# Gate times up on VectorE straight from the PSUM bank, and an instruction order planned from traced durations

## The chip, the cores and the metric

One core of one Trainium2 chip. The time is device microseconds of one execution of the kernel on that core; the time before is the median of three executions. Engines are named as in the profile: PE is TensorE's matmuls and PEld its weight loads, DVE is VectorE, ACT is ScalarE, POOL is GpSimd, SP is SyncE, whose queue issues all transfers. A wait is written as "who <- whom".

## The reference

The input is x of 4 x 2048 x 256 in f32. Two residual blocks follow each other.

1. A layer norm, and then a Mamba block with a layer norm and a residual of its own: a projection to xi and z (512 channels each), a causal convolution of four taps and Silu that give u, a projection of u to dt, B and C, delta = softplus(dt W + b), and a scan over time with 64 states for each of the 512 channels, `h = h * exp(delta * A) + delta * u * B`, `y = sum over states of h * C`. Then y + u D, times silu(z), times W_out.
2. A layer norm and a feed-forward part with hidden size 768: `silu(x Wg) * (x Wu)`, times Wd, where the weights are integers times 1/127.

```
h = jax.nn.silu(gate) * up
return jnp.einsum('bsh,dh->bsd', h, wd)
```

The change sits in this last product, and in the order of everything.

## The kernel before

**Tiling.** Time is cut into 16 blocks n of 512 tokens (4 sequences of 4 blocks). In a block the scan has 512 channels times 64 states, which is 256 tiles of 128 partitions (2 channels by 64 states) by 512 steps. Sixteen tiles make a group; there are 256 groups in all. A group lives in one of three ring buffers, `ring`, of 16 x 512 floats per partition.

**One group** (function `group`):
- SP loads delta times u, repeated over 64 partitions, from a scratch in DRAM (`dusc`) into the ring, four transfers of 1 MB, and the exponents' pieces into `stk`.
- POOL multiplies by B, eight tiles in one instruction (L1524, 8.9 us), after it put the carried state into the first column (L1409) where a sequence goes on.
- For each tile, PE spreads delta over the partitions into one of four PSUM banks `a` (L1419), ACT makes exp(A delta) of it in place (L1425), and DVE runs the scan in the ring (L1430). ACT copies the last column into `carry` (L1440).
- PE contracts the 16 tiles with C (L1454, 128 small matmuls), ACT copies that (L1474), PE sorts it (L1487), ACT copies it to `yt` (L1498). Then the ring is free.

**Dense work** of neighbouring blocks is interleaved with the groups: `front`, `front_a` and `front_b` of block n+1 (layer norms, projections, convolution, Silu of u and z at L909 to L912, `softplus`), `back` of block n-1 (the gate with z and W_out), and `back_b` of block n-1, the feed-forward part. The layer norm's statistics are DVE's (L447, L448), its root goes through four small operations on ACT that end at L469, and DVE goes on at L472. `softplus` makes on ACT and POOL (L853, L855) the two summands that PE adds in a bank (L861), ACT copies the bank (L867), and DVE multiplies it by u (L868) into one of four buffers `w2`, which SP stores to `dusc`; the buffer is written again once the store is done. L1023 is DVE's gate of the scan's result, from a bank that PE filled at L999. The four `ps` banks of PSUM are shared by all dense work and the contraction.

**The feed-forward part** (`back_b`, 15 times; the last block has a version of its own, `back_last`): six projections for the gate, evicted by ACT (L1137), one Silu over all six (L1156, L1157, with the exponential's table loaded again at L1158), and six projections for up. Each of those is copied out of its bank by ACT into a `w2` buffer (L1144), and POOL multiplies the gate by it (L1146). Then the projection down (L1055).

**What sets the order.** No engine's order is written by hand. `Planner` takes every operation with an engine, a cost in ns and what it reads and writes; `run` keeps a clock for each engine and places one operation after another, the one that can start earliest, with a bias for its due step among the scans. Instructions are issued in that order, and each engine runs its own queue in order. So each cost (`SCAN`, `dve(n)`, `act(n)`, the figures in the `op` calls, `LAT` between engines, `WIRE` in bytes per ns for transfers) moves instructions. The ring products ("MUL") go to POOL in sets of eight, or singly to DVE in the first group alone. PE gets a decay matmul twice where the planner thinks it would otherwise be too little used (L1419 runs 5248 times for 4096 tiles).

Of the kernel before, what the change touches and what calls it, by code (L numbers as in the profile page):

```python
# [21 lines left out]
T = 512  # L22
# [7 lines left out]
NPS = 4  # L30
EXP_LN = "natural_log_exp_and_others"

LAT = {"PE": 195, "ACT": 137, "DVE": 150, "POOL": 150, "SP": 0, ("ACT", "PE"): 190, ("DVE", "DVE"): 130}
SLOPE = 17.0
LEAD = 170.0
LAG = -230.0
# [14 lines left out]
HOLD_TOL = 300.0  # L51
HOLD_ON = ("PE", "ACT")
WINDOW = 0
WIRE = 300.0
SCAN = 1130
TINY = 160


def lag(src, dst):
# [28 lines left out]
class Planner:  # L88
# [105 lines left out]
    def run(self, mul):  # L194
        clock = {e: 0.0 for e in ("PE", "ACT", "DVE", "POOL", "SP")}
        busy = dict(clock)
        wire = 0.0
        cols, recent = {}, deque()
        cur = 0
        self.ready = {e: [] for e in list(clock) + ["MUL"]}  # L200
        for o in self.ops:
            if not o.wait:
                self.ready[o.eng].append(o)
        left = len(self.ops)

        def bias(o):
            if o.kind == "S":
                return 0.0
            return max(LAG, min(LEAD, SLOPE * (o.step - cur)))

        while left:
            best = None
            for e, now in clock.items():
                pick = None
                cands = []
                due = 1e18
                for o in self.ready[e]:
                    t = self.allocatable(o, 2)
                    if t is None:
                        continue  # L220
                    t = max(now, o.est, t)
                    if e == "SP" and o.kind == "S":
                        t = max(t, wire - AHEAD)
                    if o.kind == "S":
                        due = min(due, t)
                    cands.append((o, t))
                for o, t in cands:
                    late = HOLD if e in HOLD_ON and o.kind != "S" and t + o.cost > due + HOLD_TOL else 0.0
                    sc = (t + bias(o) + late, o.idx)
                    if pick is None or sc < pick[0]:  # L230
                        pick = (sc, t, [o])
                if self.ready["MUL"] and (e == "POOL" or e == "DVE" and self.ready["MUL"][0].key[0][0] == 0):
                    m = min(self.ready["MUL"], key=lambda o: o.idx)
                    whole = m.key[0][0] == 0 or MUL_SET == sum(o.key[0] == m.key[0] for o in self.ready["MUL"])
                    if e == "POOL":
                        ms = sorted(
                            (o for o in self.ready["MUL"] if o.key[0] == m.key[0]), key=lambda o: o.idx
                        )
                        ms = [o for i, o in enumerate(ms) if o.key[2] == m.key[2] + i]
                        sc = 0.0  # L240
                    else:
                        ms = [m]
                        sc = max(LAG, min(MUL_LEAD, SLOPE * (m.step - MUL_MARGIN - cur)))
                    t = max(now, max(o.est for o in ms))
                    sc = (t + sc, m.idx)
                    if whole and (pick is None or sc < pick[0]):
                        pick = (sc, t, ms)
                if pick and (best is None or pick[1] < best[1]):
                    best = (e, pick[1], pick[2])
            assert best, "no instruction can be placed"  # L250
            e, t, os = best
            if os[0].eng == "MUL":
                cost = 120 + 1092 * len(os) if e == "POOL" else 690
                mul(e, os)
                clock[e] = end = t + cost
                busy[e] += cost
                for o in os:
                    self.ready["MUL"].remove(o)
                    o.eng = e
                    self.commit(o, t, end)  # L260
                left -= len(os)
                continue
            o = os[0]
            self.ready[e].remove(o)
            cost, times = o.cost, 1
            if e == "PE":
                i = int(t / TICK)
                if cols.get(i - 1, 0) < WARM:
                    cost *= 2
                n = o.cols or o.cost * 2.4  # L270
                while recent and recent[0][0] < t - TICK:
                    recent.popleft()
                if o.key == "decay" and sum(c for _, c in recent) < KEEP:
                    times = 2
                    cost *= 2
                    n *= 2
                recent.append((t + cost, n))
                i = int((t + cost) / TICK)
                cols[i] = cols.get(i, 0) + n
            if e == "SP":  # L280
                clock[e] = t + 625
                wire = max(wire, t + 1275) + o.cost
                end = wire + 985
                busy[e] += o.cost
            else:
                clock[e] = end = t + cost
                busy[e] += cost
            if o.key == "scan":
                cur += 1
            self.commit(o, t, end)  # L290
            for _ in range(times):
                o.fn()
            left -= 1
        return clock, busy
# [25 lines left out]
def mamba_ffn_kernel(  # L320
# [74 lines left out]
    nc.gpsimd.memset(cz.rearrange("p a b c -> p (a b c)"), 0.0)  # L395

    def dve(n=T, ptr=False, fast=False):
        return 140 + n * (0.52 if fast else 1.0417) + (61 if ptr else 0)

    def act(n=T, psum=False, ptr=0):  # L400
        return n * 0.834 + (70 if psum else 110) + 93 * ptr
# [7 lines left out]
    def tok(t):  # L409
        return t.t.rearrange("p a t -> p (a t)").rearrange("p (s c) -> p s c", s=4)  # L410
# [14 lines left out]
    def layer_norm(src, blocks=range(4), twice=False):  # L425
# [18 lines left out]

        def stats(j, s):
            st = buf("bst")
            op("DVE", 402, lambda: nc.vector.bn_stats(st.t, tok(src)[:, s, :]), [(src, s // 2)], [st])  # L447
            op("DVE", TINY, lambda: nc.vector.bn_aggr(mv()[:, j, :], st.t), [st], [(lp, 0, j)])  # L448

        for j, s in enumerate(blocks):  # L450
            stats(j, s)
# [276 lines left out]
    def front_a(n):  # L728
# [4 lines left out]
        def ev_x(k):  # L733
# [4 lines left out]
            def ev(ps):  # L738
# [8 lines left out]

                def weigh(j):
                    op(
                        "PE", 1220,  # L750
                        lambda: nc.tensor.matmul(  # L751
                            ps.t, dg.t[:, j * P : (j + 1) * P], xi.t[:, j : j + T], start=(j == 0), stop=(j == 3)
                        ),
                        [(xi, 0), (xi, 1), dg], [ps],
                    )
# [78 lines left out]
    def softplus(n, m):  # L834
# [14 lines left out]
        def ev(ps):  # L849
# [7 lines left out]

            def add(t):
                op(
                    "PE", 1220,  # L860
                    lambda: nc.tensor.matmul(ps.t, ident, t.t, start=False, stop=True, skip_group_check=True),  # L861
                    [t], [ps],
                )
# [35 lines left out]
    def front_b(n):  # L899
# [3 lines left out]
        if n:  # L903
# [7 lines left out]
                    nc.scalar.activation(szs[h].t, szs[h].t, AF.Silu)  # L911
                nc.scalar.preload_act_table_set(EXP_LN)  # L912

            op("ACT", 6240, silu, uk + zk, uk + zk)
        else:

            def silu_a():
# [10 lines left out]

        def mm_dt(k):
            return (  # L930
                240,
                lambda ps: nc.tensor.matmul(
                    ps[32 * k : 32 * k + 32, :], framed(wxp, k), u.t[:, k, :], start=True, stop=True
                ),
            )
# [174 lines left out]
    def back_b(n):  # L1110
# [29 lines left out]

        def ev_u(k):
            def ev(ps):
                up = buf("w2")
                op("ACT", act(T, True), lambda: nc.scalar.copy(up.t, ps.t), [ps], [up])  # L1144
                op(
                    "POOL", 1230, lambda: nc.gpsimd.tensor_tensor(hm(k), hm(k), up.t, ALU.mult),  # L1146
                    [up, hk[k]], [hk[k]],
                )

            return ev  # L1150

# [5 lines left out]
            nc.scalar.activation(hmb.t, hmb.t, AF.Silu)  # L1157
            nc.scalar.preload_act_table_set(EXP_LN)  # L1158

        op("ACT", 5300, silu, hk, hk)  # L1160
        for k in range(6):
            project(wgu, HID + k * P, xT, ev_u(k), [("wgu", 1, k)])
        wdk = [("wd", c, k) for c in range(2) for k in range(3)]
# [160 lines left out]
    def carry_over(n, h):  # L1324
# [22 lines left out]
        def c0(j):  # L1347
# [13 lines left out]
            [ps], xk[0:2], step=at,  # L1361
        )
        op(
            "POOL", 460, lambda: nc.gpsimd.tensor_tensor(ck2, ck2, c0(0), ALU.mult),
            xk[0:2] + ck, ck, step=at,
        )
        op(
            "POOL", 460, lambda: nc.gpsimd.tensor_tensor(ck2, ck2, c0(1), ALU.add),
            xk[2:4] + ck, ck, step=at,
        )  # L1370

    def group(G):
# [32 lines left out]
                load_du(a, m)  # L1405
        if not first:
            op(
                "POOL", 250,
                lambda: nc.gpsimd.tensor_copy(ring.t[:, :, 0], carry[:, g * 16 : g * 16 + 16]),  # L1409
                [("carry", g)], heads,  # L1410
            )
# [52 lines left out]
        for hb in range(2):  # L1464
            pm = buf("ps")
            for j in range(4):
                r8 = hb * 4 + j
                op(
                    "PE", 592, unit(pm, r8), keys + czk, [pm], step=s0 + 1 + C_PACE * r8,
                    after=[last["ext"]] if "ext" in last else [], cols=1024,  # L1470
                )

            def evac(hb=hb, pm=pm):
                nc.scalar.copy(  # L1474
# [17 lines left out]
                        stop=(jl == 1),  # L1492
                    )

        last["ext"] = op("PE", 592, ext, [(mm, 0), (mm, 1), "exs"], [ex], alloc=[yt], step=s0 + 18, cols=1024)

        def put():
            nc.scalar.copy(  # L1498
# [95 lines left out]
```

## Time and profile before

| | |
|---|---|
| median of 3 executions | 5084.1 us (5080.46 to 5089.4) |
| profiled execution | 5088.69 us, span of its instructions 5086.9 us |
| granted TensorE clock, mean | 0.968 |
| DMA | 1299.85 MB, 256 GB/s over the span, queue q1 67.4% of 16 engines' time |
| steady part, 130 to 4965 us | DVE busy 4614.06, POOL 4648.86, ACT 3833.08, PE 4248.31 of 4835.0 |
| gate copies by ACT, L1144 | 90 of 594 ns |
| gate products by POOL, L1146 | 90 of 1275 ns |

How to read what follows: a group's line gives line, engine, operation, tiles written and read, shapes and count, then busy us and mean ns of one, then the engine's idle time just before them and what ended most of it. A wait's line gives the total in us, how often, and the longest. In a timeline the two first numbers are start and length in us, a bracket is idle time just before and who ended it.

### The profile page before, as it was taken

The page shows a single profiled execution, that of the slowest core. Times are in us where ns is not written, and L with a number is a line of the kernel's source. Part 1 is how long each engine was busy: PE and PEld are TensorE (multiplying, and loading weights), DVE is VectorE, ACT ScalarE, POOL GpSimd, SP SyncE. Part 2 cuts the span into 40 slices and gives each one's busy share as a digit, 9 for nine tenths or more (in the row PEclk, how much of TensorE's full clock was granted, in tenths as well). Part 3 has the DMA queues.
Part 4 walks back from the last instruction along what each step waited for, and adds up shares of the span by engine and source line. Part 5 has one row for each costly group of instructions (what it writes and reads, how often), then busy time and mean ns, then how long its engine had stood idle before and what let it go on. Part 6 is the DMA issues. An engine that isn't in the chain of part 4 may idle for free. (4 is left out here: it accounts for less than half of the span.)

```text
span 5086.9 us, 115635 instructions
## 1 busy us (share of the span) xinstructions
PE 4443.6 (87%) x46946; PEld 2210.7 (43%) x46946; DVE 4769.4 (94%) x4681; ACT 3985.9 (78%) x7158; POOL 4764.7 (94%) x917
## 2 busy tenths in 40 slices
PE   7879898998988989889998888988889898898888
PEld 3334353443534435344443544435344353443435
DVE  5999999999999999999999999998999999999996
ACT  7777878878787787877878788777887878878674
POOL 4999999999999999999999999998999999999994
PEclk8999999999999999999999999989999999999999
DMA  7666776676776667767677776667766676666762
GB/s 265 258 251 250 259 274 264 245 277 241 277 275 235 257 254 286 279 245 277 242 269 258 276 279 244 267 237 258 267 250 267 241 284 255 249 258 246 274 243 88
DMA packets 306345, 1299.85 MB, mean 256 GB/s; under 512 B 33617, under 2 KB 134737, under 8 KB 174866
## 3 DMA queue, kind: packets, MB, share of 16 engines
q1 hardware_dynamic: 305810, 1292.44, 67.4%
q8 instruction: 369, 6.05, 0.5%
q14 instruction: 166, 1.36, 0.1%
HBM read 1186.94 MB, written 105.38 MB: 254 GB/s over the span
## 5 line engine op out<-in xcount | busy, mean ns | idle before, releaser
L1430 DVE TENSOR_TENSOR_SCAN ring<-a,ring 128x512 f32<-128x512 f32 x4096 | 4599.2, 1198 | 163.1 <-ACT a L1425 104.7
L1524 POOL TENSOR_TENSOR ring<-ring,b 128x4088 f32<-128x4088 f32 (+2 forms) x512 | 4538.7, 8894 | 86.0 <-DMA ring<-dusc 59.4
L1425 ACT ACTIVATE a<-a,a 128x512 f32<-128x512 f32 x4096 | 2686.0, 665 | 749.2 <-PE a L1419 715.5
L1419 PE MATMUL a<-stk,selb 128*128 128x512 bf16 x5248 | 1846.1, 395 | 460.9 <-DVE ring L1430 423.7
L1454 PE MATMUL ps<-ring,cz 128*32 128x128 f32 x32768 | 1223.8, 280 | 27.8 <-issue 19.7
L1419 PEld LDWEIGHTS <-selb 128*128 128x128 bf16 x5248 | 495.6, 99 | 1488.9 <-issue 1390.3
L1454 PEld LDWEIGHTS ps<-ring,cz 128*32 128x32 f32 x32768 | 818.9, 110 | 587.4 <-issue 525.6
L523 PE MATMUL ps<-w,wgu 128*128 128x512 f32 x720 | 372.3, 600 | 0.1
L1474 ACT COPY mm<-ps 128x512 f32<-128x512 f32 x512 | 302.7, 592 | 71.8 <-PE ps L1454 70.7
L1487 PE MATMUL ps<-mm,exs 128*32 128x128 f32 x4096 | 285.3, 408 | 13.2 <-ACT mm L1474 12.8
L523 PE MATMUL ps<-w,win 128*128 128x512 f32 x512 | 262.2, 597 | 0.0
L751 PE MATMUL ps<-xi,w 128*128 128x512 f32 x480 | 250.7, 604 | 0.0
L1487 PEld LDWEIGHTS ps<-mm,exs 128*32 128x32 f32 x4096 | 117.0, 119 | 204.8 <-ACT a L1425 75.0
L1055 PE MATMUL ps<-wd,w 128*128 128x256 f32 x720 | 181.2, 381 | 0.0
L523 PEld LDWEIGHTS ps<-w,wgu 128*128 128x128 f32 x720 | 136.8, 192 | 96.4 <-issue 52.2
L855 POOL TENSOR_TENSOR w<-w,w 128x512 f32<-128x512 f32 x63 | 81.3, 1290 | 101.3 <-ACT w L853 101.3
L861 PE MATMUL ps<-w,ident 128*128 128x512 f32 x252 | 147.2, 669 | 31.6 <-ACT w L854 21.1
L1146 POOL TENSOR_TENSOR w<-w,w 128x512 f32<-128x512 f32 x90 | 113.2, 1275 | 42.2 <-ACT w L1144 42.1
L1055 PEld LDWEIGHTS ps<-wd,w 128*128 128x128 f32 x720 | 135.6, 190 | 31.1 <-issue 4.8
L523 PEld LDWEIGHTS ps<-w,win 128*128 128x128 f32 x512 | 98.7, 193 | 74.8 <-issue 43.4
L1055 PE MATMUL ps<-wout,w 128*128 128x256 f32 x480 | 127.0, 383 | 1.3 <-ACT ps L1070 1.0
L751 PEld LDWEIGHTS ps<-xi,w 128*128 128x128 f32 x480 | 86.5, 189 | 78.7 <-issue 70.8
(138 smaller groups left out, 2407.2 us busy)
## 6 DMA issues: line engine op xcount, KB each, us to landing
ring<-dusc SPq DMA_DIRECT2D x1023, 1024.0 KB, 7.0
stk<-dsc SPq DMA_DIRECT2D x256, 96.0 KB, 3.8
qd<-w SPq DMA_DIRECT2D x32, 512.0 KB, 8.4
szd<-w SPq DMA_DIRECT2D x32, 512.0 KB, 8.3
dusc<-w SPq DMA_DIRECT2D x63, 256.0 KB, 3.4
dsc<-pk SPq DMA_DIRECT2D x63, 256.0 KB, 3.5
rsum<-w SPq DMA_DIRECT2D x31, 512.0 KB, 4.2
w<-rsum SPq DMA_DIRECT2D x31, 512.0 KB, 7.2
```

Source lines behind the costliest of these rows:

```text
L523: lambda ps: nc.tensor.matmul(ps, w[:, c, o : o + P], xT.t[:, c, :], start=(c == 0), stop=(c == 1)),
L751: lambda: nc.tensor.matmul(ps.t, dg.t[:, j * P : (j + 1) * P], xi.t[:, j : j + T], start=(j == 0), stop=(j == 3)),
L861: lambda: nc.tensor.matmul(ps.t, ident, t.t, start=False, stop=True, skip_group_check=True),
L1055: lambda ps: nc.tensor.matmul(ps[:, (s % 2) * DM : (s % 2 + 1) * DM], src(k)[:, s * P : (s + 1) * P], w[:, k, :], start=False, stop=(k == ...
L1146: "POOL", 1230, lambda: nc.gpsimd.tensor_tensor(hm(k), hm(k), up.t, ALU.mult),
L1419: "PE", 216, lambda: nc.tensor.matmul(a.t, selb[:, p, :], stk.t, start=True, stop=True),
L1425: lambda: nc.scalar.activation(a.t, a.t, AF.Exp, scale=a2f[:, idx : idx + 1]), [a, "a2"], [a],
L1430: nc.vector.tensor_tensor_scan(v, a.t, v, 0.0, ALU.mult, ALU.add)
L1454: nc.tensor.matmul(pm.t[cg * 32 : cg * 32 + 32, (r8 % 4) * P : (r8 % 4 + 1) * P], framed(cz, blk), ring.t[:, :, blk * 8 : blk * 8 + 8], st ...
L1474: nc.scalar.copy(mm.t[:, hb * 4 : hb * 4 + 4].rearrange("p r a t -> p (r a t)"), pm.t)
L1487: nc.tensor.matmul(ex.t[jh * 32 : jh * 32 + 32, 0:P], framed(exs, jh * 2 + jl), mm.t[:, :, :, jh * 2 + jl], start=(jl == 0), stop=(jl == 1),)
L1524: e.tensor_tensor(v, v, b2.t[:, None, t0:].to_broadcast([P, m, T - t0]), ALU.mult)
```

## The change

The planner's figures are replaced: transfers at 390 bytes per ns for 300, a scan at 1115 for 1130, DVE's fixed part at 50 for 140, the layer norm's operations at 326, 205 and 60 for 402, 160 and 160, the convolution's and softplus's matmuls on PE at 860 for 1220, the Silus and some POOL operations, and a surcharge where PE goes from a decay matmul to one with narrow weights. The six up projections of `back_b` are no longer copied: DVE multiplies the gate by the bank itself. `back_last` did so already, in halves. Line numbers move: by five up to the feed-forward part (L868 becomes L873), not at all in the first part of `group` (L1425 and L1430), by two at its end (L1524 becomes L1526). The gate product is L1148.

```
-LAT = {"PE": 195, "ACT": 137, "DVE": 150, "POOL": 150, "SP": 0, ("ACT", "PE"): 190, ("DVE", "DVE"): 130}
+LAT = {"PE": 195, "ACT": 137, "DVE": 165, "POOL": 150, "SP": 0, ("ACT", "PE"): 190, ("DVE", "DVE"): 140}
...
-WIRE = 300.0
-SCAN = 1130
-TINY = 160
+WIRE = 390.0
+SCAN = 1115
+TINY = 60
+SWITCH = 90
...
-                cost = 120 + 1092 * len(os) if e == "POOL" else 690
+                cost = 88 + 1092 * len(os) if e == "POOL" else 690
...
+                if was == "decay" and o.key == "narrow":
+                    cost += SWITCH
+                was = o.key
...
-        return 140 + n * (0.52 if fast else 1.0417) + (61 if ptr else 0)
+        return 50 + n * (0.52 if fast else 1.0417) + (61 if ptr else 0)
...
-            op("DVE", 402, lambda: nc.vector.bn_stats(st.t, tok(src)[:, s, :]), [(src, s // 2)], [st])
-            op("DVE", TINY, lambda: nc.vector.bn_aggr(mv()[:, j, :], st.t), [st], [(lp, 0, j)])
+            op("DVE", 326, lambda: nc.vector.bn_stats(st.t, tok(src)[:, s, :]), [(src, s // 2)], [st])
+            op("DVE", 205, lambda: nc.vector.bn_aggr(mv()[:, j, :], st.t), [st], [(lp, 0, j)])
...
-                        "PE", 1220,
+                        "PE", 860,
...
-            op("ACT", 6240, silu, uk + zk, uk + zk)
+            op("ACT", 6400, silu, uk + zk, uk + zk)
...
-                240,
+                430,
...
         def ev_u(k):
             def ev(ps):
-                up = buf("w2")
-                op("ACT", act(T, True), lambda: nc.scalar.copy(up.t, ps.t), [ps], [up])
-                op(
-                    "POOL", 1230, lambda: nc.gpsimd.tensor_tensor(hm(k), hm(k), up.t, ALU.mult),
-                    [up, hk[k]], [hk[k]],
-                )
+                op("DVE", dve(), lambda: nc.vector.tensor_tensor(hm(k), hm(k), ps.t, ALU.mult), [ps, hk[k]], [hk[k]])
...
-        op("ACT", 5300, silu, hk, hk)
+        op("ACT", 5450, silu, hk, hk)
...
-            "POOL", 460, lambda: nc.gpsimd.tensor_tensor(ck2, ck2, c0(0), ALU.mult),
+            "POOL", 400, lambda: nc.gpsimd.tensor_tensor(ck2, ck2, c0(0), ALU.mult),
...
-                "POOL", 250,
+                "POOL", 150,
...
-                op(
-                    "PE", 592, unit(pm, r8), keys + czk, [pm], step=s0 + 1 + C_PACE * r8,
+                o = op(
+                    "PE", 560, unit(pm, r8), keys + czk, [pm], step=s0 + 1 + C_PACE * r8,
                     after=[last["ext"]] if "ext" in last else [], cols=1024,
                 )
+                o.key = "narrow"
...
-        last["ext"] = op("PE", 592, ext, [(mm, 0), (mm, 1), "exs"], [ex], alloc=[yt], step=s0 + 18, cols=1024)
+        last["ext"] = op("PE", 1045, ext, [(mm, 0), (mm, 1), "exs"], [ex], alloc=[yt], step=s0 + 18, cols=1024)
+        last["ext"].key = "narrow"
```

More of the change, by code (lines that the diff above doesn't have):

```diff
@@ L198, in run @@
         cols, recent = {}, deque()
+        was = None
         cur = 0
@@ L859, in add @@
                 op(
-                    "PE", 1220,
+                    "PE", 860,
                     lambda: nc.tensor.matmul(ps.t, ident, t.t, start=False, stop=True, skip_group_check=True),
@@ L1367, in carry_over @@
         op(
-            "POOL", 460, lambda: nc.gpsimd.tensor_tensor(ck2, ck2, c0(1), ALU.add),
+            "POOL", 400, lambda: nc.gpsimd.tensor_tensor(ck2, ck2, c0(1), ALU.add),
             xk[2:4] + ck, ck, step=at,
```

## The prediction

> **What bounds the kernel now.** I read the busy shares first, then the waits of VectorE (DVE) in the steady part, then the timeline around one place of each kind of wait. Busy shares and three groups:
>
> ```profile
> PE 4443.6 (87%) x46946; PEld 2210.7 (43%) x46946; DVE 4769.4 (94%) x4681; ACT 3985.9 (78%) x7158; POOL 4764.7 (94%) x917
> ...
> L1430 DVE TENSOR_TENSOR_SCAN ring<-a,ring 128x512 f32<-128x512 f32 x4096 | 4599.2, 1198 | 163.1 <-ACT a L1425 104.7
> L1524 POOL TENSOR_TENSOR ring<-ring,b 128x4088 f32<-128x4088 f32 (+2 forms) x512 | 4538.7, 8894 | 86.0 <-DMA ring<-dusc 59.4
> ...
> L1146 POOL TENSOR_TENSOR w<-w,w 128x512 f32<-128x512 f32 x90 | 113.2, 1275 | 42.2 <-ACT w L1144 42.1
> ```
>
> Two engines stand at 94%: DVE with the 4096 scans and GpSimd (POOL) with the products that the scans read. One follows the other through three ring buffers, so either can set the pace. A table by stage settles the steady part, 130 to 4965 us: of 4835.0 us DVE is busy 4614.1 and idle 220.9. The busy part is work that must be done; a change there is worth its duration, and everything else is worth what it takes from or adds to the 220.9. Its largest pieces, as waits of DVE in that stretch (total, times, longest):
>
> ```profile
> DVE ring L1430 <- ACT a L1425: 101.2, 61, 3.3
> DVE ring L1430 <- POOL ring L1409: 34.2, 23, 6.0
> DVE ps L472 <- ACT ps L469: 21.4, 7, 4.6
> DVE w L868 <- ACT pk L867: 15.1, 22, 2.4
> DVE w L868 <- ACT x L872: 14.2, 10, 3.3
> DVE ring L1430 <- POOL ring L1524: 7.5, 2, 3.8
> ```
>
> The first row splits by the timeline. At 15 places ScalarE runs the Silu of u and z (L909 to L912), at 15 more that of the feed-forward part (L1156 to L1158); with four `a` banks DVE runs dry there, 41.0 and 30.4 us in all. The other 29.8 us of the row are elsewhere. Most of the POOL waits (rows 2 and 6, 41.7 us) follow the second Silu. POOL there, between two sets of ring products:
>
> ```profile
> 649.40 1.27 POOL L1146 TENSOR_TENSOR w<-w,w 128x512 f32<-128x512 f32 x1
> 652.13 1.29 POOL L1146 TENSOR_TENSOR w<-w,w 128x512 f32<-128x512 f32 x1 [1.47 <-ACT w L1144]
> ...
> 654.46 8.87 POOL L1524 TENSOR_TENSOR ring<-ring,b 128x4088 f32<-128x4088 f32 x1
> 663.29 4.96 POOL L1146 TENSOR_TENSOR w<-w,w 128x512 f32<-128x512 f32 x4
> ```
>
> The reader sees six gate products in POOL's queue, one of them waiting for ScalarE's copy while ring products stand behind it. DVE then waits 0.80 us at 653.8 and 4.64 us at 673.3. POOL's lead over DVE, from the end of a ring set to its first scan, has a median of 3.9 us over the 255 later groups and falls to 0 after this place, period by period.
>
> **The change part by part.** The order of both builds, engine by engine, shows that it does what it says: 90 products move to DVE (DVE goes from 4683 to 4779 instructions, with six more ring products of the first group), 90 copies leave ScalarE, 90 products leave POOL, and 58 decay matmuls that only keep TensorE warm go.
>
> 1. Added work on DVE. A product of this form, 128x512 with one operand in a PSUM bank, lasts 688 ns (L1079). What one costs in line is less:
>
> ```profile
> 1045.48 5.66 DVE L1430 TENSOR_TENSOR_SCAN ring<-a,ring 128x512 f32<-128x512 f32 x5
> 1051.05 0.66 DVE L1023 TENSOR_TENSOR w<-ps,yl 128x512 f32<-128x512 f32 x1
> 1051.63 4.55 DVE L1430 TENSOR_TENSOR_SCAN ring<-a,ring 128x512 f32<-128x512 f32 x4
> ```
>
> Scan follows scan by 1.115 us (median of all such pairs), though one lasts 1.198; scan, product, scan is 1.697 between the scans without waits. So a product costs 0.582 us, and 90 cost **+52.4 us**. The Trainium skill ("VectorE: DVE Perf Modes", section "The DRAIN you can't avoid") states that the next operation starts only when the pipe is empty; the 1.115 against 1.198 disagrees. By that rule the price would be 90 x 0.688 = 61.9 us, 9.5 more.
> The six extra ring products (0.582 each, 3.5 us) lie before 80 us, where DVE also waits for transfers and POOL: +2, between 0 and 3.5.
>
> 2. New wait of DVE for the bank. Behind each waiting product stand the scans; behind those the `a` banks and TensorE. I counted in the order how many scans stand between the scan that frees the last decay bank ahead of the up matmul on TensorE and the product on DVE: none in 4 places, one in 22, two or more in 64. What must fit is a decay matmul (0.395), the second up matmul (0.600) and about 0.2 of signalling, 1.2 us, against 1.115 per scan. So 4 x 1.2 + 22 x 0.2 = **+9 us**; bounds 0 and 32 (the nearest rows, the L1023 products, wait 22.8 us in 64, and 90 x 0.36 = 32).
>
> 3. POOL is relieved of 113.2 us of products and 42.1 of waits in a queue that is 96% busy in the steady part (4648.9 of 4835.0). What goes on DVE are the 41.7 us, except those behind L855, which stays: **-36**, bounds -20 and -42. What is late next is the transfer: the start of a ring set comes 7.4 us at the least, 15.2 in the median, after the contraction that frees the ring, so POOL can run some 7 us further ahead before transfers stop it.
>
> 4. The layer norm's wait (L472, 21.4 us in 7). In the order before, exactly seven of these in the steady part have no scan between the last L448 and L472, so DVE stands through four operations of ScalarE. The new durations put 1, 2 or 14 scans there every time, and places with 1 or 2 do not wait now: **-21**, bounds -15 and -21.
>
> 5. Softplus's buffer. ScalarE waits 39.2 us for the store of w before it may write it again (L853), up to 4.6 us, and DVE runs dry behind it; that is most of the 29.8 us. From the scan of the store to the reuse there were five scans or fewer in 16 places and are in 5 after, six in 6 and 9. I take half: **-15**, bounds 0 and -30.
>
> 6. Waits of L868 and L1023 (30.8 and 12.6 in the steady part): distances are more even, with no clear gain; -5, bounds +20 and -20. The first gate product stands in the shadow of the second Silu in 8 of 15 places, where DVE is idle anyway: 8 x 0.582, **-5**.
>
> 7. Nothing for the 90 copies (53.1 us): ScalarE at 78% waits 715.5 us for decay matmuls, and those wait for DVE; if that cover went, the copies would be a gain of 53.1 at most. Nothing for 58 x 0.395 = 23 us of TensorE, which waits 423.7 us for scans. SP's 1904 entries are the same in number, another order of transfers; at 67.4% load I count nothing, and DMA waits of DVE were none in the steady part. The two Silus keep their 71.4 us less the 5. The tail after the last scan, 5032 to 5087, has the same operations in the same places.
>
> Sum: 52.4 + 2 + 9 - 36 - 21 - 15 - 5 - 5 = **-18.6 us**. The profiled execution took 5088.7 us (span 5086.9 and 1.8 around it), 4.6 over the median of 5084.1. So 5070.1 for an execution like the profiled one, and **5065** on the median's footing.
>
> **The rivals.**
> - *Slower.* DVE is the one bound, and waits only change cause: the POOL waits go (-36), but the new order makes as many stalls of ScalarE and TensorE as it takes away. 52.4 + 2 + 9 - 36 = +27, so 5111. It decides when less than 63 us of the 220.9 goes. For it: L868, L1023 and the Silus are not touched by the new durations. Against: the counts of points 4 and 5. 0.23.
> - *No change.* Half of points 4 to 6: -23 in place of -46, so about +4 and 5088, or 5075 to 5094 around it. 0.21.
> - *Much faster.* With POOL ahead and order and durations in step, most of the 149.5 us outside the Silus goes, say 120: 52.4 + 2 + 9 - 120 - 5 = -62, so 5022. For it: the lead of POOL that recovers. 0.13.
> - *On a rule.* The Trainium skill ("Perfetto Trace Analysis", section "Optimizing Scalar/DVE Operations") speaks against the change: when VectorE is saturated, work is to be taken off it, to ScalarE or GpSimd. The 94% of DVE agree, and by the rule alone the sum is the added products and no more, +52. The POOL wait rows are what it leaves out.
> - That the change isn't made as it says has no chance: the order shows the 90.
>
> **How the numbers follow.** Forecast 5050 to 5073: 0.43; much faster 0.13; no change 0.21; slower 0.23. Within 0.2% means 5073.9 to 5094.3, about what a measurement of this kernel can tell from no change. Faster is 0.43 + 0.13 = 0.56, same 0.21, slower 0.23. All worst ends together (52.4 + 3.5 + 32 - 20 - 15 + 20) give +73, 5157; all best (52.4 - 42 - 21 - 30 - 20 - 5) -66, 5018. The range of 5022 to 5118 leaves out the far ends of both.
>
> **What would show it.** Right: DVE busy up by about 52 to 62, its idle time in the steady part from 221 to 150; no POOL row over 10 us among DVE's waits; L472's row near 0; POOL near 92% and more of its idle time behind DMA. Wrong: a wait of the gate products on TensorE's bank well over 9 us, ScalarE's `a` row over 101.2 (ScalarE or TensorE became the pace), scans of more than 1.198 us, or a lower granted clock than 0.968.

## The result, and the profile after

The kernel became slower by 0.4%: 5105.3 us in the median of 6 runs (5101.94 to 5109.25), against 5085.1 of the kernel before (6 runs, 5080.45 to 5093.99). The ratio is 1.0039, 95% interval 1.0026 to 1.0052. The forecast was 5065, faster; the range of 5022 to 5118 held the time, the sign was wrong. The profiled execution took 5101.94 us (span 5100.1) at a granted clock of 0.974, against 5088.69 (5086.9) at 0.968.

The page after; the lines answer to the first fence of the prediction:

```profile
PE 4502.0 (88%) x46888; PEld 2159.3 (42%) x46888; DVE 4827.6 (95%) x4777; ACT 3939.5 (77%) x7068; POOL 4650.4 (91%) x827
...
L1526 POOL TENSOR_TENSOR ring<-ring,b 128x4088 f32<-128x4088 f32 (+2 forms) x512 | 4530.6, 8868 | 260.2 <-DMA ring<-dusc 185.8
L1430 DVE TENSOR_TENSOR_SCAN ring<-a,ring 128x512 f32<-128x512 f32 x4096 | 4607.2, 1194 | 110.4 <-ACT a L1425 65.0
```

DVE's busy time rose by 58.2 us. POOL fell to 91%, and its idle time ahead of the ring products went from 86.0 to 260.2 us, most of it behind the ring's loads: POOL no longer sets the pace. Before the scans DVE waits 110.4 us, not 163.1. So far everything is as forecast. The span grew by 13.2 us because 58.2 came and only 45.0 of DVE's 317.5 us of idle time went. In the steady part (130 to 4975 us after the change) its idle time fell from 220.9 us to 186.1; the prediction had named 150 as the sign of being right. None of the signs of being wrong that it named came. Where the idle time stayed, as waits of DVE from 130 to 4975 us (total, times, longest):

```profile
DVE ring L1430 <- ACT a L1425: 65.0, 51, 3.1
DVE ring L1430 <- issue: 29.0, 10, 3.2
DVE w L873 <- ACT x L877: 27.7, 20, 2.2
DVE w L873 <- ACT pk L872: 17.4, 13, 3.2
DVE ring L1430 <- POOL ring L1409: 11.9, 16, 2.5
DVE w L873 <- PE ps L866: 10.4, 9, 2.9
DVE w L1028 <- ACT mm L1475: 7.4, 9, 1.7
DVE w L1148 <- PE ps L528: 4.6, 8, 1.5
DVE ring L1430 <- POOL ring L1526: 3.0, 3, 1.5
```

Rows 5 and 9, the POOL waits, are 14.9 us for 41.7 (the larger is 11.9, where the prediction had none over 10); the layer norm's row (L472, now L477) is gone. The row "issue" is no new cause: nine of its ten waits lie at the Silu of u and z, once in a block, while ScalarE loads the exponential's table. What grew is softplus's product on DVE, L873: rows 3, 4 and 6 are 55.5 us, and the same rows of L868 were 30.8. They wait mostly for ScalarE, as the scans do, and part of the time ScalarE itself waits for a store. That wait among the waits of ScalarE, before:

```profile
ACT w L853 <- DMA dusc<-w: 39.2, 21, 4.6
```

and after:

```profile
ACT w L858 <- DMA dusc<-w: 46.7, 25, 4.9
```

The prediction had counted half of what this wait costs DVE as gained. What one such wait does is seen at 1470 us. SP's timeline after, transfers as they are issued:

```profile
1469.58 1.40 SPq L409 DMA_DIRECT2D ring<-dusc  x2
1477.74 0.33 SPq L412 DMA_DIRECT2D dusc<-w  x1
```

ScalarE's after, from the same place on:

```profile
1478.29 0.59 ACT L890 CAST pk<-ps 128x512 bf16<-128x512 f32 x1
1483.76 0.63 ACT L858 ACTIVATE w<-w 128x512 f32<-128x512 f32 x1 [4.88 <-DMA dusc<-w]
1484.30 0.64 ACT L1425 ACTIVATE a<-a,a 128x512 f32<-128x512 f32 x1
...
1490.64 0.66 ACT L1425 ACTIVATE a<-a,a 128x512 f32<-128x512 f32 x1 [1.95 <-PE a L1419]
```

TensorE's:

```profile
1487.68 2.07 PE L866 MATMUL ps<-w,ident 128*128 128x512 f32 x2 [4.86 <-ACT w L859]
1489.55 1.91 PE L1419 MATMUL a<-stk,selb 128*128 128x512 bf16 x4
```

and DVE's:

```profile
1477.02 0.69 DVE L873 TENSOR_TENSOR w<-ps,w 128x512 f32<-128x512 f32 x1 [1.31 <-ACT x L877]
1477.62 4.56 DVE L1430 TENSOR_TENSOR_SCAN ring<-a,ring 128x512 f32<-128x512 f32 x4
1484.97 4.56 DVE L1430 TENSOR_TENSOR_SCAN ring<-a,ring 128x512 f32<-128x512 f32 x4 [2.79 <-ACT a L1425]
1491.39 1.22 DVE L1430 TENSOR_TENSOR_SCAN ring<-a,ring 128x512 f32<-128x512 f32 x1 [1.86 <-issue]
```

DVE makes softplus's product at 1477.0 and SP issues its store at 1477.74, behind ring loads of which at least two are still in flight; it lands 5.7 us later. The next softplus tile writes the buffer again (L858), and ScalarE stands for 4.88 us until the store has landed. The exponentials of the scan stand behind it in ScalarE's queue, so DVE uses up its four `a` banks and waits 2.79. Softplus's sum (L866) stands ahead of the decay matmuls (L1419) in TensorE's queue, so these come late too and DVE waits 1.86 once more (the tenth wait of the row "issue"). One late store costs DVE 4.65 us in two places, and neither row names the store.

### The profile page after: what moved, and what is told of

Its sections match the earlier page's. It is cut to its first block, busy times and chain, and to the rows that moved or that the text cites. A ratio compares the mean times of both kernels' runs of the same rounds, so it can differ in the third digit from the quotient of the medians.

```text
span 5100.1 us, 115505 instructions
## 1 busy us (share of the span) xinstructions
PE 4502.0 (88%) x46888; PEld 2159.3 (42%) x46888; DVE 4827.6 (95%) x4777; ACT 3939.5 (77%) x7068; POOL 4650.4 (91%) x827
## 5 line engine op out<-in xcount | busy, mean ns | idle before, releaser
L1526 POOL TENSOR_TENSOR ring<-ring,b 128x4088 f32<-128x4088 f32 (+2 forms) x512 | 4530.6, 8868 | 260.2 <-DMA ring<-dusc 185.8
L1430 DVE TENSOR_TENSOR_SCAN ring<-a,ring 128x512 f32<-128x512 f32 x4096 | 4607.2, 1194 | 110.4 <-ACT a L1425 65.0
L1425 ACT ACTIVATE a<-a,a 128x512 f32<-128x512 f32 x4096 | 2697.5, 665 | 871.5 <-PE a L1419 843.8
L1419 PE MATMUL a<-stk,selb 128*128 128x512 bf16 x5190 | 1831.9, 391 | 435.6 <-DVE ring L1430 386.2
L1454 PE MATMUL ps<-ring,cz 128*32 128x128 f32 x32768 | 1301.4, 281 | 30.0 <-ACT yt L1500 23.6
L1454 PEld LDWEIGHTS ps<-ring,cz 128*32 128x32 f32 x32768 | 795.1, 110 | 774.0 <-issue 688.2
L1419 PEld LDWEIGHTS <-selb 128*128 128x128 bf16 x5190 | 479.0, 98 | 1363.8 <-issue 1284.2
L866 PE MATMUL ps<-w,ident 128*128 128x512 f32 x252 | 143.7, 654 | 59.3 <-ACT ps L861 37.4
L1060 PE MATMUL ps<-wd,w 128*128 128x256 f32 x720 | 192.3, 383 | 0.0
L1060 PEld LDWEIGHTS ps<-wd,w 128*128 128x128 f32 x720 | 134.8, 190 | 34.7 <-issue 7.2
L860 POOL TENSOR_TENSOR w<-w,w 128x512 f32<-128x512 f32 x63 | 80.4, 1277 | 65.6 <-ACT w L858 65.6
L528 PEld LDWEIGHTS ps<-w,win 128*128 128x128 f32 x512 | 95.2, 191 | 67.4 <-issue 44.0
L503 ACT ACTIVATE w<-w,s,s 128x256 f32<-128x256 f32 x192 | 111.1, 592 | 0.7 <-DVE s L487 0.6
## 6 DMA issues: line engine op xcount, KB each, us to landing
szd<-w SPq DMA_DIRECT2D x32, 512.0 KB, 13.2
```

The costliest lines, as they stand in the source:

```text
L503: lambda: nc.scalar.activation(tok(dst)[:, s, :], tok(src)[:, s, :], AF.Identity, bias=nm.t[:, o + s : o + s + 1], scale=rs.t[:, ro + s : ...
L528: lambda ps: nc.tensor.matmul(ps, w[:, c, o : o + P], xT.t[:, c, :], start=(c == 0), stop=(c == 1)),
L1060: lambda ps: nc.tensor.matmul(ps[:, (s % 2) * DM : (s % 2 + 1) * DM], src(k)[:, s * P : (s + 1) * P], w[:, k, :], start=False, stop=(k == ...
L1419: "PE", 216, lambda: nc.tensor.matmul(a.t, selb[:, p, :], stk.t, start=True, stop=True),
L1425: lambda: nc.scalar.activation(a.t, a.t, AF.Exp, scale=a2f[:, idx : idx + 1]), [a, "a2"], [a],
L1430: nc.vector.tensor_tensor_scan(v, a.t, v, 0.0, ALU.mult, ALU.add)
```

## The experiments

All times are medians with the kernel before run on the same chip; "against before" is the ratio's distance from 1 times 5082 us. The change has two parts that can be had apart, the products and the costs.

**The products alone.** The kernel before with this one edit:

```
-up = buf("w2")
-op("ACT", act(T, True), lambda: nc.scalar.copy(up.t, ps.t), [ps], [up])
-op("POOL", 1230, lambda: nc.gpsimd.tensor_tensor(hm(k), hm(k), up.t, ALU.mult), ...)
+op("DVE", dve(), lambda: nc.vector.tensor_tensor(hm(k), hm(k), ps.t, ALU.mult), [ps, hk[k]], [hk[k]])
```

> The kernel before with one edit: the six up products by VectorE from the bank; all costs of the planner as before. Theory A (the products cost VectorE 90 x 0.582 = 52 us and up to 58, and give back the waits for GpSimd, 27 to 42): 10 to 31 us over the kernel before. Theory B (the products are about even, the new costs do the harm): within 8 us of the kernel before. In both VectorE's waits for GpSimd fall from 41.7 us to under 20, and the layer norm's wait (21.4 us) may stay.

5077.4 us, ratio 0.9991 (0.9981 to 1.0001): 5 us under before, which the interval does not tell from no change. Theory A (10 to 31 us over before) was missed. Theory B's number came, but the next run shows that its reason, harm by the new costs, is wrong.

**The costs alone.** The changed kernel with the same edit undone.

> The changed kernel with the six products back as copies by ScalarE and products by GpSimd, and all new costs kept. Theory A (the costs take 21 us of layer-norm waits and give back about 25 in softplus's product): within 8 us of the kernel before, with the waits for GpSimd still near 40. Theory B (the new costs do the harm): 12 to 25 us over the kernel before.

5043.1 us, ratio 0.9923 (0.9909 to 0.9936): 39 us faster. Both expectations were missed: neither theory had the costs gain. So the parts are worth -5 and -39 alone and +20 together; they work against each other by 64 us. The wait of ScalarE for the store, with the costs alone:

```profile
ACT w L858 <- DMA dusc<-w: 6.9, 8, 2.2
```

It is nearly gone here and 49.0 us in the products alone. The POOL waits of DVE are the other way round: 51.3 us between the first and the last scan with the costs alone, 13.6 with the products alone.

**Every second product only.** The changed kernel, with the copy and POOL's product again where `k % 2` is 1. It was made to see whether POOL's relief comes with the first products taken away, and whether the store's wait goes with the number of products on DVE.

> The changed kernel with every second up product (45 of 90) back at ScalarE's copy and GpSimd. Theory A (VectorE's work is the price, GpSimd needs only part of the relief): 45 x 0.582 = 26 us less work on VectorE and GpSimd's waits under 25 us, so 10 to 25 us under the changed kernel. Rival (each product that waits in GpSimd's queue holds up a ring set, whether three or six stand there): within 8 us of the changed kernel.

5110.3 us, ratio 1.0057 (1.0045 to 1.007). Theory A's number was missed and its rival's was hit by the medians (5 us from the changed kernel; 9 by the ratios): three products on DVE bring no relief of POOL. DVE's waits in this run:

```profile
DVE ring L1438 <- ACT a L1433: 83.1, 47, 3.4
DVE ring L1438 <- POOL ring L1417: 45.1, 31, 6.9
...
DVE ring L1534 <- DMA ring<-dusc: 9.2, 3, 4.2
DVE ring L1438 <- POOL ring L1534: 7.5, 6, 2.8
```

The second and the last row are 52.6 us, as much as with six products on POOL. ScalarE's wait for the store is 45.1, against 46.7 with all six on DVE, so it does not go with the number of products.

**Another order of ScalarE's copies.** In 20 places DVE's product waits behind ScalarE's copy of `x0` (L877); both read one bank. The copy was made to come behind the product:

```
-... nc.scalar.copy(x0.t[:, 0, :, i], ps.t[:, 0:1].to_broadcast([P, 64])), [ps], [(x0, 0, i)])
+... nc.scalar.copy(x0.t[:, 0, :, i], ps.t[:, 0:1].to_broadcast([P, 64])), [ps, w], [(x0, 0, i)])
```

> The changed kernel, where softplus's copy of the bank's first column by ScalarE (L877) is made to come behind VectorE's product (L873), as 48 of 63 places need it at all. Theory A (VectorE waits behind ScalarE's reads of the same bank, which the planner has no cost for; 27.7 us of its waits name this copy): the L873 waits fall from 55.5 us to 25 to 35 and the time by 10 to 25 us under the changed kernel. Rival (the product would wait for TensorE's sum or the other copy of the bank anyway): the row goes to another name, and the time stays within 6 us of the changed kernel.

5155.9 us, ratio 1.0142 (1.0128 to 1.0156). Both expected times were missed: 72 us slower than before. The copy's row went, and the product waits 56.3 us for L872, the copy of the bank, instead, as the rival had it. ScalarE's wait:

```profile
ACT w L858 <- DMA dusc<-w: 72.7, 26, 6.5
```

With this run the theory fell that the place of this copy is the loss. The slowest kernel of all has the longest wait for the store, and that turned the search to it. By then the waits for the store were 6.9 at 5043, 39.2 at 5085, 46.7 at 5105, 45.1 at 5110 and 72.7 at 5156; but 49.0 at 5077 speaks against a plain proportion.

**How much of this is chance of the order.** A cost changed by 1 ns gives another order of the same work. `SCAN` went from 1115 to 1116 in the changed kernel and in the costs alone, and from 1130 to 1131 in the products alone.

> The changed kernel with the planner's cost of a scan at 1116 for 1115 ns and nothing else: the same instructions in another order. Theory C (the order is so sensitive that any cost moves the time by tens of us, and the sum of the two halves, -40 and -5, against the whole, +20, is within that scatter): 10 us or more away from the changed kernel's 5105, on either side. Theory D (products on VectorE and new costs work against each other by a mechanism that every such order has): within 8 us of 5105.

> The kernel with the new costs alone (products on GpSimd) and the scan's cost at 1116 ns. Theory C: 10 us or more away from its 5043. Theory D: within 8 us of 5043.

> The kernel with the products on VectorE alone (old costs) and the scan's cost at 1131 for 1130 ns. Theory C: 10 us or more away from its 5077. Theory D: within 8 us of 5077.

5099.1 (ratio 1.0038, 1.0025 to 1.0052), 5031.5 (0.9906, 0.989 to 0.9923) and 5063.9 us (0.9966, 0.9955 to 0.9978). By the ratios the three move by less than 1, by 9 and by 13 us from their neighbours: Theory D holds for the whole change, Theory C for the products alone, and the costs alone lie between the two. So an edit that moves the order cannot be read to less than some 13 us here, from three pairs. The 64 us by which the parts work against each other stand well above that, and in the neighbouring orders they are 84 (-48 and -17 apart, +19 together). The wait for the store keeps its pattern too: 52.3 us in the whole change at 1116, 2.9 in the costs alone at 1116, 31.3 in the products alone at 1131. 5031.5 is the fastest kernel of the study, 0.9% under before.

**A buffer of its own for the store.** What the wait for the store costs is told by taking away what makes ScalarE wait: softplus's product is written into a buffer `yl` and stored from there, so that `w` is free as soon as DVE has read it. The changed kernel with:

```
-op("DVE", dve(), lambda: nc.vector.tensor_tensor(w.t, ps.t, u.t[:, k, :], ALU.mult), [ps, (u, k)], [w])
-store(dusc[r][h][i], lambda: w.t, 262144, [w], [("dusc", r, h, i)])
+du = buf("yl") if n > 1 else w
+op("DVE", dve(), lambda: nc.vector.tensor_tensor(du.t, ps.t, u.t[:, k, :], ALU.mult), [ps, (u, k)], [du])
+store(dusc[r][h][i], lambda: du.t, 262144, [du], [("dusc", r, h, i)])
```

and the second copy of `x0` reading `du`.

> The changed kernel, where softplus's product for blocks 2 to 15 is written to and stored from one of the two yl buffers, which nothing else uses at that time, in place of the w2 buffer that ScalarE writes again soon. In the changed kernel ScalarE waits 46.7 us for that store; in the kernel with the costs alone hardly at all. Theory E (that wait, through ScalarE's exponentials and softplus's chain, is what the two halves together lose): the wait falls under 8 us and the time by 20 to 40 us, to 5065 to 5085. Rival (ScalarE's wait lies in the shadow of something else): the wait goes and the time stays within 8 us of 5105.

5055.2 us, ratio 0.9951 (0.9936 to 0.9966): 45 us under the changed kernel by the ratios, more than Theory E expected; the rival (within 8 us) fell. The wait of ScalarE in this kernel:

```profile
ACT w L858 <- DMA dusc<-w: 1.9, 2, 1.0
```

Its stores, by the DMA issues (count, KB, median us to landing):

```profile
dusc<-yl SPq DMA_DIRECT2D x56, 256.0 KB, 6.1
```

They take 6.1 us to land, against 5.4 in the changed kernel. The store got no faster; nobody waits for it. DVE's first row, the scans behind ScalarE, went from 65.0 to the first line here, and the rows of softplus's product from 55.5 us to 26.2 in all, the two largest of them in the other lines:

```profile
DVE ring L1431 <- ACT a L1426: 46.4, 31, 3.0
DVE yl L874 <- ACT x L878: 11.6, 9, 2.0
DVE yl L874 <- PE ps L866: 8.8, 8, 2.2
```

These two falls are 48 us together, and the time fell by 45.

**The same buffer in the other three kernels.** If the wait is the cause, the buffer must give nothing where the wait was already gone (the costs alone), and then the two parts must add up.

> The new costs alone (products on GpSimd), with softplus's product stored from a yl buffer of its own as in the run before it. Theory E (the buffer's wait is what the whole change has and the costs alone lack): the costs alone waited almost nothing there, so the time stays within 12 us of 5031 to 5043, the two orders measured of it. Then the 5055 of the whole change with its own buffer leaves 10 to 25 us for the products by themselves. Rival (a buffer of its own helps every order by some 50 us): 4985 to 5000.

> The products on VectorE alone (old costs), with softplus's product stored from a yl buffer of its own. Its two orders waited 49 and 31 us for that store on ScalarE at 5077 and 5064 us. Theory E: 15 to 40 us less than their mean, 5030 to 5055. Rival: within 10 us of that mean, 5070.

> The kernel before with softplus's product stored from a yl buffer of its own and nothing else. It waits 39.2 us for that store on ScalarE, and VectorE waits 29.8 us for exponentials outside the Silus. Theory E: 15 to 35 us under the kernel before. Rival (GpSimd sets the pace there, so what ScalarE gains is lost behind GpSimd): within 8 us of the kernel before.

Against before, with the ratio's interval of the runs with the buffer:

| | store from `w` | store from `yl` | ratio with `yl` |
|---|---|---|---|
| before | 0 | -40 | 0.9922 (0.9904 to 0.994) |
| costs alone | -39, at 1116 -48 | -45 | 0.9911 (0.9894 to 0.9927) |
| products alone | -5, at 1131 -17 | -29 | 0.9942 (0.9927 to 0.9957) |
| the whole change | +20, at 1116 +19 | -25 | 0.9951 (0.9936 to 0.9966) |

(medians 5041.0, 5035.3, 5051.5 and 5055.2 us.) The buffer is worth 40 in the kernel before, nothing within the scatter with the costs alone, 12 to 24 with the products alone and 45 with both. Theory E's time was hit with the costs alone and with the products alone, and its rival (some 50 us in every order) fell. The price of the wait is not fixed: 39.2 us of it were worth 40 in the kernel before and 46.7 worth 45 in the whole change, but 49.0 and 31.3 only 24 and 12 with the products alone. In the right column the costs are worth -5 and, with the products, +4: nothing that stands above the scatter. The products are worth +11 and +20. The sum of the parts is +6, the whole change +15: of the 64 us by which they worked against each other 9 are left, less than the scatter. Each cell with the buffer is one order, and the buffer lets the planner place other operations too. The expectation for the kernel before was exceeded (15 to 35 expected, 40 measured).

**A fifth `a` bank.** The largest waits left are those behind the two Silus, where four banks run dry. In the costs alone with the buffer, `NA` went from 4 to 5 and the shared banks `NPS` from 4 to 3.

> The new costs alone with the store's own buffer, and five decay banks and three of the shared ones in place of four and four. The Silus leave VectorE dry for 61 to 75 us in every run, 30 times, once its four banks are used up. If the banks set that, one more is worth up to 30 x 1.115 = 33 us, and the Silus' row falls to 30 to 45 us: 5000 to 5020. Rival (three shared banks hold up dense work and the contraction): no gain or a loss of up to 30 us.

5075.1 us, ratio 0.999 (0.9981 to 1.0): 40 us slower than without. The expected time (5000 to 5020) was missed, and the loss was larger than the rival's 30 us. The waits of DVE in it:

```profile
DVE ring L1436 <- POOL ring L1415: 67.8, 38, 4.9
DVE ring L1436 <- POOL ring L1532: 34.2, 27, 3.5
DVE ring L1436 <- ACT a L1431: 32.8, 27, 2.5
```

The waits at the Silus fell from 61.9 to 34.7 us as expected, and those for POOL rose from 44 to 102 us. The bank was taken from the dense work and the contraction, which then come later; that this is what frees the rings late and holds POOL is argued from the rows, not tried.

## Why the prediction was wrong

**The mechanism.** Softplus's store holds the buffer that ScalarE must write next. When it lands late, ScalarE, TensorE and DVE stand one behind the other. Of the 39 us that the costs are worth alone, all but 5 go with this wait, by the table: where the store has a buffer of its own they are worth 5, less than the scatter. With the products on DVE as well, the new order brings the wait back, and the change is left with the price of the products.

Why the costs alone avoid it is seen in two counts from the traces. First the landing. By the number of 1-MB ring loads in flight when the store is issued, its time from issue to landing after the change was 2.06 us with none (11 of 58 stores), 5.12 with one (17), 6.15 with two (25) and 6.94 with three (5). With the costs alone 32 of 53 stores meet none and land in 2.02. Before the change it was 2.38, 3.12 and 5.07 with none, one and two, so the number of loads alone does not set it. Second the distance from the store's product to the next use of its buffer, in scans between them in the order: nine in 29 of 46 places with the costs alone, six to eight in 34 of 46 in the whole change. ScalarE works about two scans ahead of DVE, so it comes to the buffer sooner than the scans would take. Medians from the start of the product, over the 46 places:

| us after the product starts | before | after | costs alone |
|---|---|---|---|
| ScalarE is ready to write the buffer | 5.0 | 5.6 | 7.6 |
| the store has landed (where the trace tells it, 37 to 40 places) | 4.8 | 6.2 | 4.4 |

The reuse did move later with the change, but the landing moved more. With the costs alone the reuse is far behind the landing. The medians of the page show the first count in one line each, with the costs alone

```profile
dusc<-w SPq DMA_DIRECT2D x63, 256.0 KB, 2.4
```

and after

```profile
dusc<-w SPq DMA_DIRECT2D x63, 256.0 KB, 5.4
```

(3.4 before). The ring loads of 1 MB themselves took 7.0 us in the median before, 8.1 after and 8.2 with the costs alone. That the place in SP's order decides the store's landing is a reading of these traces; no run moved the store alone.

**Point by point.**

- *1, added work, +52.4 and +2:* right. Scan, product, scan is 1.694 us in the median, scan and scan 1.115: 0.579 a product, against the 0.582 forecast. The Trainium skill's rule weighed at this point ("VectorE: DVE Perf Modes", section "The DRAIN you can't avoid") would have it cost its whole duration, 0.663 in the mean of L1148; the trace disagrees, as before. That section excepts a next operation that is not held, so it is the rule read without that exception that the trace speaks against.
- *2, the wait for the bank, +9:* right in kind, 5.8 us in the steady part, 4.6 of them for TensorE. The 0.2 us of signalling in its sum is the planner's figure; no row gives it by itself.
- *3, POOL's relief, -36:* 41.7 went to 14.9, so -27; within the bounds, 9 short. With three of the six products on DVE nothing of it came.
- *4, the layer norm, -21:* right in the number, 21.4 to 0. With the costs alone it goes as well (1.8 us left), but also with the old costs and the products on DVE (3.0 left, none at 1131). So any of these new orders took it away; that the new durations did it is not shown.
- *5, softplus's buffer, -15:* **the step that failed.** "From the scan of the store to the reuse there were five scans or fewer in 16 places and are in 5 after, six in 6 and 9. I take half." The wait rose from 39.2 to 46.7. The count looked at the distance alone and took the time to land as fixed. The distance grew as counted (ScalarE ready 5.0 us after the product before, 5.6 after), but the time from issue to landing rose from 3.4 to 5.4 us in the median. DVE's waits for exponentials outside the Silus, which this point priced, went from 33.8 us to 23.2 with the row "issue" counted in (-11, not -15); with the store's own buffer they are 4.6, and 1.5 with the costs alone. Behind it stands a sentence of point 7: "SP's 1904 entries are the same in number, another order of transfers; at 67.4% load I count nothing". The longer landing is measured; that the other order of transfers brought it is read from the traces.
- *6, L868 and L1023, -5 and -5:* L868's rows are +24.7 in place of a small gain, L1023's -2.6: +22 for the -5, beyond the +20 of its bounds and the largest miss of a row. It is part of the chain of point 5: with the store's own buffer softplus's product waits 26.2 us between the first and last scan, 33.5 before and 55.5 after. Of the Silu shadow's 5 next to nothing came: the waits there went from 71.4 to 70.8. In these rows points 5 and 6 together missed by 36 us and point 3 by 9; the whole forecast was off by 39 (-18.6 to +20).
- *7, nothing for the copies, TensorE and the tail:* as forecast, as far as the runs tell: ACT's busy time fell by 46 us; no run took the copies away alone.

**Which rival came.** *Slower*, "waits only change cause", had 0.23 and 5111; measured were 5105. It named ScalarE's stalls without the store, and it kept the layer norm's wait, which went (-21) while softplus's product rose by as much (+25): its number is in part luck. With the store's buffer out of the way, the working of points 1 to 3 for the products, 52.4 + 2 + 9 - 36 - 5 for the Silu shadow, gives +22; the runs gave +11 and +20. The Trainium skill ("Perfetto Trace Analysis", section "Optimizing Scalar/DVE Operations") says that it may make sense to take work off a saturated VectorE. That has the sign right for the products where the store has its own buffer; the +52 that the prediction drew from it is more than twice what they cost there. In the kernel before as it stands, with the old costs, the products gave -5 and -17.

**What stays open.** Why the planner, with the new costs, sets softplus's products 14 to 17 scans apart in 41 of 45 places with the gate products on POOL, and 9 to 11 apart in 26 of 45 with them on DVE: that POOL is freer in its plan and takes L860 earlier is a guess, not tried.

## What to carry to other kernels

A buffer that a store still holds is a wait of the engine that writes it next, and its price moves with the order of the transfers: weigh distance to the reuse against the time from issue to landing behind the loads in flight, not distance alone, or give the store a buffer of its own. In a kernel whose order is planned, run each part of a change alone before its value is told, and once with a cost changed by 1 ns to see the scatter. Work given to an engine at 95% costs less than its duration when it ends waits of that engine: here 52 us of products cost 11 and 20 once no other wait came with the new order.

## What the runs showed of the hardware

- After the change a 256-KB store landed in 2.1 us with no 1-MB load seen in flight, and in 5.1, 6.2 and 6.9 us with one, two and three (medians), at a mean load of the queue of 67%. In the kernel before, at the same load, it was 2.4 us with none and 3.1 and 5.1 with one and two.
- A VectorE product of 128x512 with an operand in PSUM lasts 0.66 to 0.69 us and costs 0.58 between scans; a scan lasts 1.194 to 1.200 in the runs' means and follows the one before by 1.115.
- 1 ns in a planned cost of 1115 or 1130 moved the ratio to the kernel before by 0.01% to 0.25%, up to 13 us.
